# Attention and FFN kernel: w1 moved in two halves, the last batch's rows turned on VectorE, Wq loaded between rows B and C

## The chip, the cores and the metric

The kernel runs on one core of a Trainium2 chip. Its time is that of one launch on the device, in microseconds (us). Five engines work side by side, each through its own list of instructions in order: TensorE (PE; PEld is its loading of weights), VectorE (DVE), ScalarE (ACT), GpSimd (POOL) and SyncE (SP). They wait for one another by semaphores. Transfers are issued by an engine's queue (here SP's and, a few, ACT's) and carried out by 16 DMA engines.

## What is computed

```python
xn = layernorm(x)                                  # x: (8, 1024, 128)
Q = einsum('bnd,hdk->bhnk', xn, proj_q)            # 8 heads
K = einsum('bmd,dk->bmk', xn, proj_k)              # one K and one V for all heads
V = einsum('bmd,dv->bmv', xn, proj_v)
O = softmax(Q @ K.T) @ V
attn = einsum('bhnv,hdv->bnd', O, proj_o)
mid = einsum('amh,ehn->aemn', xn, w1)              # 8 experts, w1: (8, 128, 512)
ffn = einsum('aemn,enh->amh', mid, w2)             # w2: (8, 512, 128)
out = x + attn + ffn
```

All of it is in 32-bit floats. Nothing stands between the two FFN products, so the kernel multiplies w1 and w2 together once, into a 128x128 matrix `wf`. It likewise folds the key projection into the query weights (`wqk`) and the output projection into the values (`wvo`).

## The kernel before, in words

**The unit of work.** The main loop has 512 turns (`for i in range(NS)`): 8 batches of 8 heads of 8 blocks of 128 queries. In turn i, `logits(i)` multiplies the block of queries with all 1024 rows: eight matmuls into a PSUM tile `pl`, of which two exist (tag `sc`, shared with the tiles for queries and values). `exponents(i)` takes the row maximum on VectorE (`nmax`, L359) and the exponents and their sums on ScalarE (`e`, L362). `weights_t(i - 1)` turns the weights of the turn before on VectorE (L394), in 32x32 blocks, into a tile `turned`; `divide(i)` takes the reciprocal of the sums (VectorE, L371) and multiplies (ScalarE, L372).

**From weights to products.** VectorE's transposition works inside 32x32 blocks. Once four turns have filled a `turned` tile (half of a head, 2 MB), `move_blocks` puts the blocks in their places by 16 moves of 32 partitions x 4 KB, issued by SP (L410): the first tile of a head into `g0`, the second into `g1`. There are two buffers of `turned`, two of `g0` and one of `g1`. Twelve turns after a head's first turn (`LAG`), `pair` and `product` multiply `g0`, `g1` and sums of them that GpSimd makes (`f1`, `f4`, L425 to L433) with the values `vf`, into four PSUM banks `acc0` to `acc3` (L455). In the last turns of the kernel TensorE turns the weights instead (`weights_t_pe`).

**Order.** It is written out by hand: every engine gets its instructions in the order in which the program text issues them, and SP's DMAs too stand in one queue in that order.

**The head** (L159 to L173 and the calls before the loop). ACT's queue loads wk, the first head of wq, and the other seven heads (L164). SP's queue loads x_0 in four pieces of two chunks (rows A to D, L163), then wv, wo, w1 (2 MB, into `w1s`, which has the buffer of `g0`) and w2 in two parts. The rows are normalized and turned on TensorE pair by pair (`xn_t_pair`, `pxn`). TensorE turns wq in two groups (`wq_part(1, 4)`, `wq_part(4, 8)`, tile `pwq`) that are copied by ScalarE, multiplies it with wk (`wqk_product`), and does a few products of zeros (`keep_clock`, tile `pidle`). Four PSUM banks are handed out in rotation (`bank`). The rest of the preparation is spread over the first turns by the table `early`.

**w1.** In turns 0 to 3 `turn_w1(k)` turns a quarter of `w1s` on VectorE (L225) into `w1_turned`, part of the buffer of the first values. After the fourth, `load_rows(1)` loads the rows of batch 1 and `move_w1` issues 16 moves of 32 partitions x 4 KB back into `w1s` (L234). In turns 8 to 11 `ffn_weights(k)` multiplies eight of 32 chunks each into `pwf` (bank `acc3`), ScalarE copies the sum (L244), and turn 12 turns it on TensorE (`pwf_t`) and copies it into `wf`.

**Rows of the later batches.** `load_rows(b)` loads them, VectorE takes the moments, GpSimd normalizes. For batches 1 to 6 VectorE turns them (`turn_rows`, L273, one transposition of 1024 columns) and SP moves the blocks in four groups of four moves, four turns apart (`move_rows`, L282). The columns of `xnT` then stand in an order of their own. For the last batch TensorE turns the eight chunks in one go (`xn_t`, L296) and ScalarE copies them (L297), in the natural order.

Of the kernel before, what the change touches and what calls it, by code (L numbers as in the profile page):

```python
# [9 lines left out]
F32 = mybir.dt.float32  # L10
# [7 lines left out]
def kernel(  # L18
# [42 lines left out]
    nc = tc.nc  # L61
    ctx.enter_context(tc.manual_schedule())
    P = 128
# [4 lines left out]
    B, S, D = x.shape  # L68
    H = proj_q.shape[0]
    NE, _, NF = w1.shape  # L70
    NB = S // P
    GN = 4
    GS = GN * P
    NFC = NF // P
    Q = 32
    NQ = P // Q
# [7 lines left out]
    batch = ctx.enter_context(tc.tile_pool(name="batch", bufs=2))  # L84
# [7 lines left out]
    def blocks(t):  # L92
        return t.rearrange("p (c d) -> p c d", d=P)

    def slot(name):
        return ps_sc.tile([P, S], F32, tag="sc", name=name)

    banks, pwf = [0], []

    def both_halves(dst, lhsT, rhs, start=True, stop=True):  # L100
        for half in range(2):
            r = ts(half, HP)
            nc.tensor.matmul(dst[r], lhsT=lhsT[:, r], rhs=rhs, start=start, stop=stop)  # L103

    def bank(name):

        banks[0] = (banks[0] + 1) % (3 if pwf else 4)
        return ps_acc.tile([P, GS], F32, tag=f"acc{banks[0]}", name=name)
# [52 lines left out]
    x_0 = late.tile([P, NB, D], F32, tag="x", name="x_0")  # L161
    for i in range(GN):
        nc.sync.dma_start(x_0[:, ts(i, 2)], chunked(x[0])[:, ts(i, 2)])  # L163
    nc.scalar.dma_start(wq[:, 1:], proj_q[1:].rearrange("h d k -> d h k"))  # L164
    nc.sync.dma_start(wv, proj_v)
    nc.sync.dma_start(wo, proj_o.rearrange("h d v -> d h v"))
    nc.sync.dma_start(w1s.rearrange("p (e n) -> p e n", e=NE), w1.rearrange("e h n -> h e n"))
# [30 lines left out]
    def transposed(dst, srcs, name, copy):  # L198

        pt = blocks(bank(name))  # L200
        for c, src in enumerate(srcs):
            nc.tensor.transpose(pt[:, c, :], src, ident)
        copy(dst, pt[:, : len(srcs), :])

    def wqk_product(first, n):
        pt = blocks(bank(f"pwqk_{first}"))
        if first == 0:
            nc.tensor.matmul(pt[:, 0, :], lhsT=wqT[:, 0, :], rhs=wkT, start=True, stop=True)
        else:
            for c in range(n):  # L210
                both_halves(pt[:, c, :], wqT[:, first + c, :], wkT)
        nc.scalar.copy(wqk[:, first : first + n, :], pt[:, :n, :])
# [4 lines left out]
        nc.scalar.copy(wvo[:, ts(g, GN), :], blocks(pt))  # L217

    wfT = s_v[:, :P]
    w1T = w1s.rearrange("p (r i a) -> p r i a", r=NQ, a=Q)  # L220

    def turn_w1(k):

        i = ts(k, NB)
        nc.vector.transpose(  # L225
            w1_turned.rearrange("p (k i a) -> p i k a", k=NQ, a=Q)[:, i],
            w1s.rearrange("p (i k q) -> p i k q", k=NQ, q=Q)[:, i],
        )

    def move_w1():  # L230
        n = NE * NFC * Q
        for r in range(NQ):
            for k in range(NQ):
                nc.sync.dma_start(w1s[ts(k, Q), ts(r, n)], w1_turned[ts(r, Q), ts(k, n)])  # L234

    def ffn_weights(k):
        if k == 0:
            pwf.append(ps_acc.tile([P, GS], F32, tag="acc3", name="pwf"))
        n = NE * NFC
        for i in range(8 * k, 8 * k + 8):  # L240
            w2_i = w2s[2 * i // n][:, i % (n // 2)]
            both_halves(pwf[0][:, :P], w2_i, w1T[:, :, i, :], i == 0, i == n - 1)
        if k == 3:
            nc.scalar.copy(wfT, pwf.pop()[:, :P])  # L244

# [29 lines left out]
            xns.pop(b).rearrange("p c (k q) -> p c k q", q=Q),  # L275
        )

    def move_quarters(dst, src, r):

        n = S // NQ  # L280
        for k in range(NQ):
            nc.sync.dma_start(dst[ts(k, Q), ts(r, n)], src[ts(r, Q), ts(k, n)])  # L282

    def move_rows(b, r):

        if r == 0:
            xnTs[b] = batch.tile([P, S], F32, tag="xnT", name=f"xnT_{b}")
        move_quarters(xnTs[b], turned_rows[b], r)
        if r == NQ - 1:
            del turned_rows[b]  # L290

    def xn_t(b):
        xnTs[b] = batch.tile([P, S], F32, tag="xnT", name=f"xnT_{b}")
        pt = slot(f"pxn_{b}")
        for c in range(NB):
            nc.tensor.transpose(pt[:, ts(c, P)], xns[b][:, c, :], ident)  # L296
        nc.scalar.copy(xnTs[b], pt)  # L297

    def xn_t_pair(k, copy):

        if k == 0:
            xnTs[0] = batch.tile([P, S], F32, tag="xnT", name="xnT_0")
        pt = bank(f"pxn_0_{k}")
        for c in range(2):
            nc.tensor.transpose(pt[:, ts(c, P)], xns[0][:, 2 * k + c, :], ident)
        copy(xnTs[0][:, ts(k, 2 * P)], pt[:, : 2 * P])

    def queries(u, first=0, last=S, copy=nc.scalar.copy):
        b, h = divmod(u, H)
        if first == 0:  # L310
            qTs[u] = work.tile([P, S], F32, tag="qT", name=f"qT_{u}")
        n = last - first
        pq = slot(f"pq_{u}") if n == S else bank(f"pq_{u}_{first}")
        for c in range(0, n, GS):
            w = min(GS, n - c)
            both_halves(pq[:, c : c + w], wqk[:, h, :], xnTs[b][:, first + c : first + c + w])
        copy(qTs[u][:, first:last], pq[:, :n])  # L317
# [30 lines left out]
    def logits_half(i, g):  # L348
        u, n = divmod(i, NB)
        if g == 0:  # L350
            pls[i] = slot(f"pl_{i}")
        both_halves(
            pls[i][:, ts(g, GS)], qTs[u][:, ts(n, P)], xnTs[u // H][:, ts(g, GS)]
        )
# [293 lines left out]
    def one(t):  # L648
        return t.rearrange("p (c x) -> p c x", c=1)

    def wq_part(first, last):
        transposed(
            wqT[:, first:last], [wq[:, h] for h in range(first, last)], f"pwq_{first}", nc.scalar.copy
        )

    def wo_part(g):
        heads = range(g * GN, (g + 1) * GN)
# [3 lines left out]
    def keep_clock(*widths):  # L661

        for n in widths:
            nc.tensor.matmul(  # L664
                pidle[:, :n], lhsT=idle[:, :P], rhs=idle[:, :n], start=True, stop=True
            )

    def norm_pair(k):
        normalize(0, x_0, nc.vector, (2 * k, 2 * k + 1))

    def stats_pair(k):
# [15 lines left out]
    xn_t_pair(1, nc.scalar.copy)  # L687
    stats_pair(2)
    queries(0, 0, P)
    keep_clock(P)  # L690
    stats_pair(3)
    logits_half(0, 0)
    norm_pair(2)
    xn_t_pair(2, nc.scalar.copy)
    norm_pair(3)
    wq_part(1, 4)
    xn_t_pair(3, nc.vector.tensor_copy)
    logits_half(0, 1)
    wq_part(4, 8)
    queries(0, P, GS)  # L700
    exponents(0)

    early = {
        0: [lambda: wqk_product(1, 3), lambda: queries(0, GS, S)],
        1: [
            lambda: wqk_product(4, 4),
            lambda: queries(1, 0, GS),
# [10 lines left out]
        9: [lambda: ffn_weights(1)],  # L718
        10: [lambda: ffn_weights(2)],
        11: [lambda: ffn_weights(3)],  # L720
        12: [lambda: transposed(one(wf), [wfT], "pwf_t", nc.scalar.copy)],
    }

    PAIRS = (2, 2, 1, 2)
# [24 lines left out]
    for i in range(NS):  # L749
        m = i % GN  # L750
        if i > 0:
            logits(i)
        for task in early.get(i, ()):
            task()
        if 0 <= i - 1 < NS - GN:
            weights_t(i - 1)
        divide(i)
        if i < 4:
            turn_w1(i)
        if i == 3:  # L760
            load_rows(1)
            move_w1()


        v, n = divmod(i - LAG, NB)
        if n == 6 and v + 1 >= 0:
            sum_early(v + 1)


        if i >= LAG:  # L770
            run(PAIRS[m] + (n == 0 and v % H == H // 2 + 1) * 2)
            if n == 0:
                sums_late(v, nc.gpsimd)
        if NS - GN <= i - 1:
            weights_t_pe(i - 1)

        if i % NB == 0 and i > 0 and i // NB + 1 < B * H:
            queries(i // NB + 1)
        if i % NB == GN and i >= LAG:
            s, r = divmod(i + 20, 32)  # L780
            if s < 2 * B:
                values(s, r // NB)


        if i == 8:
            load_x(0)
        if i == NS // B:
            ones_of_last_rows()
        for b in range(1, B):
            r = i - FIRST_ROWS if b == 1 else i - (b - 2) * H * NB - 44  # L790
            if r in ROWS:
                ROWS[r](b)
            r = i - 20 if b == 1 else i - (b - 1) * H * NB
            if b == B - 1:
                if r == 3:
                    xn_t(b)
            elif r in (0, 4, 8, 12):
                if r == 0:
                    turn_rows(b)
                move_rows(b, r // 4)  # L800
        b, r = divmod(i - 23, H * NB)
        if r == 0 and b < B:
            row_diff(b)


        b, r = divmod(i - 69, H * NB)
        if 0 <= b:
            for n in COLLECT.get(r, ()):
                collect(b, n)
            if r in (15, 19, 23, 27):  # L810
                if r == 15:
                    turn_out(b)
                move_out(b, (r - 15) // 4)
            elif r == 36:
                finish(b)
            elif r == 39:
                store(b)
            elif r == 43:
                load_x(b + 1)
# [44 lines left out]
```

## Time and profile before

| | us |
|---|---|
| median of 3 runs (lowest, highest) | 1925.15 (1924.63, 1925.58) |
| the profiled execution | 1924.67 |
| its span, first to last instruction | 1922.9 |
| TensorE busy | 1913.3 |
| SP's issues of `g <- turned`, count; median of one | 2032; 0.590 |
| landing of such a move after its issue, median | 2.4 |
| landing of w1 (2 MB) after its issue | 11.7 |

The profile shows one execution. Its page gives busy times by engine, the chain of work that ended last, and groups of instructions by source line, with the idle time before them and what ended it. Line numbers (L410) are those of the kernel before. A line such as `pl<-xnT,qT` names the tile written and the tiles read. A matmul of 32-bit floats appears as two or more records, and matmuls are pipelined: one lasts longer than the distance from its start to the next one's. A timeline has the start in us from the first instruction, the length of a merged group, engine, line, operation, shapes and count, and in square brackets the idle time before it and what ended it. `SPq` is the issuing of DMAs by SP's queue, not the transfer.

### The profile page before, as it was taken

The page shows a single profiled execution, that of the slowest core. Times are in us where ns is not written, and L with a number is a line of the kernel's source. Part 1 is how long each engine was busy: PE and PEld are TensorE (multiplying, and loading weights), DVE is VectorE, ACT ScalarE, POOL GpSimd, SP SyncE. Part 2 cuts the span into 40 slices and gives each one's busy share as a digit, 9 for nine tenths or more (in the row PEclk, how much of TensorE's full clock was granted, in tenths as well). Part 3 has the DMA queues.
Part 4 walks back from the last instruction along what each step waited for, and adds up shares of the span by engine and source line. Part 5 has one row for each costly group of instructions (what it writes and reads, how often), then busy time and mean ns, then how long its engine had stood idle before and what let it go on. Part 6 is the DMA issues. An engine that isn't in the chain of part 4 may idle for free.

```text
span 1922.9 us, 26882 instructions
## 1 busy us (share of the span) xinstructions
PE 1913.3 (100%) x9037; PEld 665.6 (35%) x9037; DVE 1397.6 (73%) x1774; ACT 1357.4 (71%) x1829; POOL 1405.8 (73%) x593
## 2 busy tenths in 40 slices
PE   9999999999999999999999999999999999999998
PEld 4444443333333333333333333333333333333333
DVE  7767778767786777777777767876777776777775
ACT  7677777777776777777777777776777776777763
POOL 2787777778676886777967778767787676677764
PEclk9999999999999999999999999999999999999999
DMA  7776676676766766677667676666766667567673
GB/s 207 173 157 147 142 155 155 150 164 151 158 144 153 169 155 142 153 159 166 141 154 158 148 176 142 149 153 150 183 139 137 148 155 169 132 143 158 150 166 87
DMA packets 138074, 295.08 MB, mean 153 GB/s; under 512 B 36816, under 2 KB 70352, under 8 KB 137936
## 3 DMA queue, kind: packets, MB, share of 16 engines
q1 hardware_dynamic: 136192, 292.50, 67.8%
q8 instruction: 73, 1.20, 0.3%
q10 hardware_dynamic: 1744, 0.85, 0.2%
q14 instruction: 65, 0.53, 0.1%
HBM read 13.76 MB, written 4.19 MB: 9 GB/s over the span
## 4 chain that ended last, share of the span: by engine, by line
PE 94%; DVE 2%; SPq 2%; ACT 1%; DMA 1%; issue 0%; ACTq 0%; DVEq 0%
PE pl L103 44%; PE acc L455 39%; PE pq L103 5%; PE pv L103 5%; SPq L410 1%; DVE nmax L359 1%; ACT e L362 1%; PE acc L488 1%; SPq L234 0%; DMA g<-turned 0%; DVE turned L394 0%; ACT e L372 0%; DMA scratch_turned<-in_L_attn_proj_q_dram 0%; PE pidle L664 0%; PE pe L383 0%
## 5 line engine op out<-in xcount | busy, mean ns | idle before, releaser
L103 PE MATMUL pl<-xnT,qT 128*64 128x512 f32 x4096 | 968.8, 593 | 2.7 <-ACT e L362 1.6
L359 DVE TENSOR_REDUCE nmax<-pl 128x1 f32<-128x1024 f32 x512 | 626.5, 1224 | 413.3 <-PE pl L103 412.5
L362 ACT ACTIVATE e<-pl,nmax 128x1024 f32<-128x1024 f32 x512 | 570.2, 1114 | 405.5 <-DVE nmax L359 405.5
L455 PE MATMUL acc<-g,vf 128*64 128x512 f32 x2560 | 852.9, 592 | 0.2 <-DMA g<-turned 0.2
L372 ACT ACTIVATE e<-e,rinv 128x1024 f32<-128x1024 f32 x512 | 588.2, 1149 | 120.1 <-DVE rinv L371 120.0
L394 DVE STREAM_TRANSPOSE turned<-e 128x1024 f32<-128x1024 f32 x508 | 628.8, 1238 | 15.1 <-DMA g<-turned 4.3
L103 PEld LDWEIGHTS pl<-xnT,qT 128*64 128x64 f32 x4096 | 299.5, 137 | 579.1 <-issue 528.5
L455 PE MATMUL acc<-f,vf 128*64 128x512 f32 x1016 | 487.2, 592 | 0.0
L430 POOL TENSOR_TENSOR g<-g,g 128x2048 f32<-128x2048 f32 x63 | 286.9, 4555 | 273.7 <-DMA g<-turned 142.7
L455 PEld LDWEIGHTS acc<-g,vf 128*64 128x64 f32 x2560 | 253.0, 137 | 504.4 <-issue 498.8
L425 POOL TENSOR_TENSOR f<-g 128x2048 f32<-128x2048 f32 x63 | 287.0, 4555 | 172.8 <-DMA g<-turned 93.5
L433 POOL TENSOR_TENSOR f<-g,g 128x2048 f32<-128x2048 f32 x63 | 287.3, 4561 | 4.9
L431 POOL TENSOR_TENSOR g<-f,g 128x2048 f32<-128x2048 f32 x63 | 286.8, 4553 | 0.0
L455 PEld LDWEIGHTS acc<-f,vf 128*64 128x64 f32 x1016 | 139.1, 137 | 0.0
L103 PE MATMUL pq<-xnT,wqk 128*64 128x512 f32 (+1 forms) x516 | 121.6, 589 | 0.0
L103 PE MATMUL pv<-wvo,xnT 128*64 128x512 f32 x512 | 120.9, 592 | 0.0
L371 DVE RECIPROCAL rinv<-sums 128x1 f32<-128x1 f32 x512 | 83.9, 164 | 48.5 <-ACT e L362 5.6
L362 ACT ACTIVATION_READ_ACCUMULATOR e<-pl,nmax 128x1 f32 x512 | 98.3, 192 | 0.0
L337 POOL TENSOR_TENSOR vf<-vf 128x256 f32<-128x256 f32 x64 | 46.8, 731 | 28.0 <-ACT vf L336 27.9
L317 ACT COPY qT<-pq 128x1024 f32<-128x1024 f32 (+2 forms) x67 | 64.0, 955 | 0.2 <-PE pq L103 0.2
L103 PEld LDWEIGHTS pv<-wvo,xnT 128*64 128x64 f32 x512 | 37.7, 137 | 72.2 <-issue 68.5
L103 PEld LDWEIGHTS pq<-xnT,wqk 128*64 128x64 f32 x516 | 37.8, 137 | 70.3 <-issue 69.7
(108 smaller groups left out, 536.0 us busy)
## 6 DMA issues: line engine op xcount, KB each, us to landing
g<-turned SPq DMA_DIRECT2D x2032, 128.0 KB, 2.4
xn<-in_L_attn_x_dram SPq DMA_DIRECT2D x7, 512.0 KB, 4.6
out<-yt SPq DMA_DIRECT2D x112, 32.0 KB, 1.9
xnT<-xnt SPq DMA_DIRECT2D x96, 32.0 KB, 1.9
x<-in_L_attn_x_dram SPq DMA_DIRECT2D x6, 512.0 KB, 4.3
out_dram<-x SPq DMA_DIRECT2D x6, 512.0 KB, 5.3
scratch_g<-in_L_ffn_w_dram SPq DMA_DIRECT2D x1, 2048.0 KB, 11.7
scratch_g<-scratch_vf SPq DMA_DIRECT2D x16, 128.0 KB, 2.4
```

The costliest lines, as they stand in the source:

```text
L103: nc.tensor.matmul(dst[r], lhsT=lhsT[:, r], rhs=rhs, start=start, stop=stop)
L317: copy(qTs[u][:, first:last], pq[:, :n])
L359: nc.vector.reduce_max(nmax, pl, AX.X, negate=True)
L362: nc.scalar.activation(es[i], pl, AF.Exp, bias=nmax, accum_out=sums[i])
L371: nc.vector.reciprocal(rinv, sums.pop(i))
L372: nc.scalar.mul(es[i], es[i], rinv)
L394: nc.vector.transpose(turned[k].rearrange("p k c t q -> p c k t q")[:, :, :, j, :], es.pop(i).rearrange("p (c k q) -> p c k q", k=NQ, q=Q),)
L425: nc.gpsimd.tensor_add(f1s[u], key_half(g0s[u], 0), key_half(g0s[u], 1))
L430: engine.tensor_sub(x1, y1, x1)
L431: engine.tensor_sub(x2, f1s[u], y1)
L433: engine.tensor_sub(f4s[u], y2, x2)
L455: nc.tensor.matmul(accs[b, acc][ts(half, HP)], lhsT=vfs[u // GN][:, u % GN, f, c, :], rhs=w[:, :, c, :], start=(h == 0 and c == first), st ...
```

## The change

- The load of the seven heads of wq leaves ACT's queue and stands in SP's, after the second of the four pieces of x_0.
- w1's turned quarters are laid out in two halves. `move_w1(j)` moves one half, 16 moves of 32 partitions x 2 KB: the first in turn 1, after two quarters have been turned, the second in turn 3, after the load of batch 1's rows. The products read w1 by halves.
- `xn_t` goes. The last batch's rows are turned by VectorE and moved by SP at the same turns of the batch as the others', but each piece of 32 columns is put in its natural place, so a move has 256 pieces of 128 B.
- In the head, the first group of wq turns takes the place of one `keep_clock` product, the second stands after the last rows instead of after the second half of the first logits; their copies and the first `wqk_product` are placed accordingly. `pwf_t` moves from turn 12 to turn 13 and takes bank `acc2` by name.

```diff
     for i in range(GN):
         nc.sync.dma_start(x_0[:, ts(i, 2)], chunked(x[0])[:, ts(i, 2)])
-    nc.scalar.dma_start(wq[:, 1:], proj_q[1:].rearrange("h d k -> d h k"))
+        if i == 1:
+            nc.sync.dma_start(wq[:, 1:], proj_q[1:].rearrange("h d k -> d h k"))
...
     def turn_w1(k):
-        i = ts(k, NB)
-        nc.vector.transpose(
-            w1_turned.rearrange("p (k i a) -> p i k a", k=NQ, a=Q)[:, i],
-            w1s.rearrange("p (i k q) -> p i k q", k=NQ, q=Q)[:, i],
-        )
+        j, first = k // 2, k % 2 * NB
+        src = w1s.rearrange("p (i k q) -> p i k q", k=NQ, q=Q)[:, ts(k, NB)]
+        dst = w1_turned.rearrange("p (j k i a) -> p j i k a", j=2, k=NQ, a=Q)
+        nc.vector.transpose(dst[:, j, first : first + NB], src)
 
-    def move_w1():
-        n = NE * NFC * Q
+    def move_w1(j):
+        n = NE * NFC * Q // 2
         for r in range(NQ):
             for k in range(NQ):
-                nc.sync.dma_start(w1s[ts(k, Q), ts(r, n)], w1_turned[ts(r, Q), ts(k, n)])
+                nc.sync.dma_start(
+                    w1s[ts(k, Q), ts(j * NQ + r, n)], w1_turned[ts(r, Q), ts(j * NQ + k, n)]
+                )
...
         for k in range(NQ):
-            nc.sync.dma_start(dst[ts(k, Q), ts(r, n)], src[ts(r, Q), ts(k, n)])
+            dst, src = xnTs[b][ts(k, Q)], turned_rows[b][ts(r, Q), ts(k, n)]
+            if b < B - 1:
+                nc.sync.dma_start(dst[:, ts(r, n)], src)
+            else:
+                dst = dst.rearrange("p (c r q) -> p r c q", r=NQ, q=Q)[:, r]
+                nc.sync.dma_start(dst, src.rearrange("p (c q) -> p c q", q=Q))
...
     queries(0, 0, P)
-    keep_clock(P)
+    turn_wq(1, 4)
     stats_pair(3)
     logits_half(0, 0)
+    copy_wq(1, 4)
     norm_pair(2)
     xn_t_pair(2, nc.scalar.copy)
     norm_pair(3)
-    wq_part(1, 4)
     xn_t_pair(3, nc.vector.tensor_copy)
+    turn_wq(4, 8)
     logits_half(0, 1)
-    wq_part(4, 8)
+    copy_wq(4, 8)
+    wqk_product(1, 3)
     queries(0, P, GS)
     exponents(0)
 
+    def turn_wf():
+        pt = ps_acc.tile([P, P], F32, tag="acc2", name="pwf_t")
+        nc.tensor.transpose(pt, wfT, ident)
+        nc.scalar.copy(wf, pt)
...
-        0: [lambda: wqk_product(1, 3), lambda: queries(0, GS, S)],
+        0: [lambda: queries(0, GS, S)],
...
-        12: [lambda: transposed(one(wf), [wfT], "pwf_t", nc.scalar.copy)],
+        13: [turn_wf],
...
         if i < 4:
             turn_w1(i)
+        if i == 1:
+            move_w1(0)
         if i == 3:
             load_rows(1)
-            move_w1()
+            move_w1(1)
...
-            if b == B - 1:
-                if r == 3:
-                    xn_t(b)
-            elif r in (0, 4, 8, 12):
+            if r in (0, 4, 8, 12):
                 if r == 0:
                     turn_rows(b)
                 move_rows(b, r // 4)
```

More of the change, by code (lines that the diff above doesn't have):

```diff
@@ L219 @@
     wfT = s_v[:, :P]
-    w1T = w1s.rearrange("p (r i a) -> p r i a", r=NQ, a=Q)
+    w1T = w1s.rearrange("p (j r i a) -> p j r i a", j=2, r=NQ, a=Q)
     def turn_w1(k):
-        i = ts(k, NB)
-        nc.vector.transpose(
-            w1_turned.rearrange("p (k i a) -> p i k a", k=NQ, a=Q)[:, i],
-            w1s.rearrange("p (i k q) -> p i k q", k=NQ, q=Q)[:, i],
-        )
-    def move_w1():
-        n = NE * NFC * Q
+        j, first = k // 2, k % 2 * NB
[4 more added lines that the diff above has]
+        n = NE * NFC * Q // 2
         for r in range(NQ):
             for k in range(NQ):
-                nc.sync.dma_start(w1s[ts(k, Q), ts(r, n)], w1_turned[ts(r, Q), ts(k, n)])
+                nc.sync.dma_start(
+                    w1s[ts(k, Q), ts(j * NQ + r, n)], w1_turned[ts(r, Q), ts(j * NQ + k, n)]
+                )
     def ffn_weights(k):
@@ L241, in ffn_weights @@
             w2_i = w2s[2 * i // n][:, i % (n // 2)]
-            both_halves(pwf[0][:, :P], w2_i, w1T[:, :, i, :], i == 0, i == n - 1)
+            both_halves(pwf[0][:, :P], w2_i, w1T[:, 2 * i // n, :, i % (n // 2), :], i == 0, i == n - 1)
         if k == 3:
@@ L276, in turn_rows @@
         )
-    def move_quarters(dst, src, r):
-        n = S // NQ
-        for k in range(NQ):
-            nc.sync.dma_start(dst[ts(k, Q), ts(r, n)], src[ts(r, Q), ts(k, n)])
     def move_rows(b, r):
@@ L287, in move_rows @@
             xnTs[b] = batch.tile([P, S], F32, tag="xnT", name=f"xnT_{b}")
-        move_quarters(xnTs[b], turned_rows[b], r)
+        n = S // NQ
+        for k in range(NQ):
+            dst, src = xnTs[b][ts(k, Q)], turned_rows[b][ts(r, Q), ts(k, n)]
[4 more added lines that the diff above has]
+                nc.sync.dma_start(dst, src.rearrange("p (c q) -> p c q", q=Q))
         if r == NQ - 1:
             del turned_rows[b]
[L292 to L297, printed above, removed]
     def xn_t_pair(k, copy):
@@ L649, in one, with turn_wq, copy_wq @@
         return t.rearrange("p (c x) -> p c x", c=1)
[L651 to L654, printed above, removed]
+    pwqs = {}
+    def turn_wq(first, last):
+        pwqs[first] = blocks(bank(f"pwq_{first}"))
+        for h in range(first, last):
+            nc.tensor.transpose(pwqs[first][:, h - first, :], wq[:, h], ident)
+    def copy_wq(first, last):
+        nc.scalar.copy(wqT[:, first:last], pwqs.pop(first)[:, : last - first])
     def wo_part(g):
```

## The prediction

> **What bounds the kernel now.** I read part 1 of the page, then what TensorE waited for, then the stretch from 15 to 66 us engine by engine. Part 1:
>
> ```profile
> PE 1913.3 (100%) x9037; PEld 665.6 (35%) x9037; DVE 1397.6 (73%) x1774; ACT 1357.4 (71%) x1829; POOL 1405.8 (73%) x593
> ```
>
> TensorE is busy for all but some 10 us of 1922.9. So a matmul that goes is worth its own length, and any other edit only matters where TensorE stands still. The view of waits on TensorE names those places (us in total, times, longest):
>
> ```profile
> PE pl L103 <- ACT e L362: 1.6, 2, 1.0
> PE pwf_t L202 <- ACT scratch_vf L244: 0.8, 1, 0.8
> PE pl L103 <- DVE xnT L306: 0.6, 1, 0.6
> ```
>
> One `pl` wait of 1.0 lies at 1891, at the end. The other, and `pwf_t`'s, lie in turns 12 and 13 of the main loop. The timeline of TensorE there (start, length, what, idle before):
>
> ```profile
> 53.80 1.95 PE L103 MATMUL pwf<-scratch_g,scratch_f 128*64 128x128 f32 x32
> 56.32 1.94 PE L103 MATMUL pl<-xnT,qT 128*64 128x512 f32 x8 [0.57 <-ACT e L362]
> 59.03 0.33 PE L202 MATMUL pwf_t<-ident,scratch_vf 128*128 128x128 f32 x1 [0.78 <-ACT scratch_vf L244]
> 59.56 1.94 PE L455 MATMUL acc<-g,vf 128*64 128x512 f32 x8 [0.20 <-DMA g<-turned]
> ```
>
> A `pl` or a `pwf` group normally takes 1.72 us from its start to the next one's, so `pl` at 56.32 is 0.80 late (53.80 + 1.72 = 55.52) and `pwf_t` 1.0 late (56.32 + 1.72 = 58.04). Both wait for ScalarE, and ScalarE waits for VectorE, whose timeline shows the cause:
>
> ```profile
> 47.11 1.23 DVE L359 TENSOR_REDUCE nmax<-pl 128x1 f32<-128x1024 f32 x1 [1.43 <-PE pl L103]
> 52.61 1.25 DVE L394 STREAM_TRANSPOSE turned<-e 128x1024 f32<-128x1024 f32 x1 [4.28 <-DMA g<-turned]
> ```
>
> The transpose at 52.61 is that of turn 8 (I call it T8). It writes `turned_2`, the third of four-turn tiles in a pool of two buffers, so it needs the buffer of `turned_0`, and that is free when the 16 moves `g0 <- turned_0` have landed. The last of them landed at 52.20. They stand in SP's queue, in order:
>
> ```profile
> 15.34 5.27 SPq L124 DMA_DIRECT2D xn<-in_L_attn_x_dram  x1
> 29.27 10.11 SPq L234 DMA_DIRECT2D scratch_g<-scratch_vf  x16
> 39.48 22.29 SPq L410 DMA_DIRECT2D g<-turned  x32
> ```
>
> SP idles from 20.6 to 29.27 (it waits for the fourth turn of w1), then issues 16 moves of w1 and 32 of `g` without a gap, 0.635 us each. **That queue sets the one stall of the main loop**, and the change rewrites it.
>
> **w1 in two halves.** 16 moves of 128 KB become 32 of 64 KB. The price of one is that of its issue: moves of 128 KB have a median of 0.590 us, those of 32 KB (`xnT <- xnt`, also 32 rows) 0.589, so I take 0.635 with the gap for 64 KB too. The sum for SP's queue:
> - Start: after turn 2 of w1, which ended at 20.78. The load of w1 landed at 15.59 and the transpose started at 15.61, so w1's landing leads here, not TensorE; I take 20.7.
> - First half, 16 moves: 10.16 (29.27 to 39.43 in this trace), to 30.86.
> - The load of xn_1 now comes here: 0.63 (the six later ones issue in 0.58 to 0.59), to 31.49. It lands by about 36 (4.6 to landing) and is read at 44.4, so the move itself is free.
> - Second half: 10.16, to 41.65. SP's moves to `g0`: 0.05, then as now 10.93 with one slow issue of 1.40, to 52.63. The last is issued at 51.98, against 49.76 now: 2.2 later.
>
> The halves are needed by `pwf` at turns 8 and 10 (41.67 and 50.34) and land by 33.3 and 44.1: no stall there, and none was there before. So the split removes no wait of TensorE and puts 17 more issues (10.8 us) before `g0` into a hole of 8.6.
>
> Then comes a second delay. At 43.3 and 53.0 the instruction queue of part 3 fetches 16 KB, every 250 or so TensorE instructions; both times the SP issue at that moment took 1.40 and 1.83 us instead of 0.59, and the moves issued up to 1.3 us before it landed late (issued 51.67 and 52.31: 4.07 and 3.75 us to landing, not 2.4). Now the second fetch hits `g1`, which has time. After the change TensorE reaches that instruction at about 53.0 - 0.92 (its lead, below) + 0.4 (four instructions fewer before it, at 0.107) = 52.5, half a us after the last `g0` move is issued. That move then lands like the one at 52.31, 3.06 after the fetch: 55.56. T8 starts 0.41 after the landing, as now (52.20 to 52.61): 55.97. **T8 is 3.36 late**; without the hit it is 51.98 + 2.85 = 54.83, 2.2 late.
>
> What follows T8 (reciprocals, exponents, the copy of `pwf`) moves with it. TensorE's `pl` goes from 56.32 to 59.68. `pwf_t` leaves turn 12, but the `acc` product in its place takes `acc3`, the bank of `pwf`, so it still waits for the copy at L244 and starts at 59.03 + 3.36 instead of 59.56 + 3.36: 0.53 gained. `pwf_t` comes back in turn 13 for about 0.2 (eight transposes took 1.12, plus an edge). Sum of turns 8 to 13: 3.36 - 0.53 + 0.20 = **+3.03**. The products with `g1` then start at 67.8; its last move lands by 66, and `f1` and `x1` on GpSimd have over 2 us left, so nothing else becomes late.
>
> **Head of the kernel.** wq's load leaves ACT's queue (0.46, ahead of a table load that ends at 3.45, while ScalarE's first work starts at 4.35 behind VectorE: nothing) and enters SP's between rows B and C (0.52). Rows C and D, wv, wo, w1 and w2 are issued 0.5 later. Rows C and D landed at 6.52 and 7.40, sharing the engines with wq, which landed at 8.13. Behind wq the same bytes are 448 + 128 + 128 KB from about 3.8 on; at 250 to 310 KB a us they end at 6.1 to 6.7: not later than now, so no cost; if they came 0.5 later, the lead below shrinks by that. TensorE: the spare matmul at 7.98 becomes three turns of wq in the same wait for ScalarE; `pxn_3` comes forward over `pwq` (-0.33: 9.92 instead of 10.25), and four turns of wq move from after `pl` into the wait before it (-0.59: 12.24 to 12.83). TensorE leads by 0.92 from turn 1. That lead is worth nothing: it ends in the wait for T8, which TensorE does not set. The price of the cover is in the third rival.
>
> **Last batch.** Eight transposes on TensorE go:
>
> ```profile
> 1440.90 0.59 PE L455 MATMUL acc<-f,vf 128*64 128x512 f32 x1
> 1441.43 1.09 PE L296 MATMUL pxn<-ident,xn 128*128 128x128 f32 x8
> 1442.45 1.94 PE L103 MATMUL pl<-xnT,qT 128*64 128x512 f32 x8
> ```
>
> Without them `pl` starts at 1440.90 + 0.43 = 1441.33: **-1.12**, all of it TensorE's own time. A copy of 0.99 on ScalarE goes with them. One transpose of 1.25 on VectorE and 16 moves on SP come; the batch before has just these at 1200 to 1254, and TensorE is busy 15.00 of 15.00 us there. The last batch writes its rows in pieces of 128 B, 256 to a move; no data piece in this trace is so small. Nearest row: the 256 pieces of 512 B of `x` (L139) issue in 0.45 to 0.58, no dearer. Upper end: 1.86, the slowest `xnT` move, for all 16; SP's stretches there are almost full (0.3 to 2.9 us free of 15), and a group's moves have some 3.6 us to spare before the transpose two groups on, so this end costs up to 2 us. I take 0, by the nearest row; first reader is turn 428, 120 us after the last move. [...]
>
> **Sum.** +3.03 - 1.12 = +1.91. Against the profiled execution (1924.67, span 1922.9) 1926.6; the median of the runs is 0.48 above it, so 1925.15 + 1.9 = **1927.1**. That is 0.1%; a measurement of this kernel tells apart about 0.2%, 3.85 us.
>
> **Rivals.**
> 1. *The fetch misses the last `g0` moves.* T8 2.2 late: 2.2 - 0.33 - 1.12 = +0.75, 1925.9. The hit rests on an estimate good to half a us. If the slow issue of 1.40 also falls elsewhere, -0.1: 1925.0. Chance 0.33.
> 2. *The clock falls* (slower). TensorE would stand from 54.83 (55.75 now, less 0.92) to 59.68, 4.85 us. This trace shows what a pause does (window, length, PE, PEld, DVE, ACT, POOL, granted clock, DMA, GB/s):
>
> ```profile
> 1918.40:1921.70 3.30, 0.00 (x0) 0.00 (x0) 0.42 (x2) 0.00 (x0) 0.00 (x0) 1.00 0.58 161
> 1921.80:1922.80 1.00, 0.00 (x0) 0.00 (x0) 0.00 (x0) 0.00 (x0) 0.00 (x0) 0.50 0.00 0
> ```
>
>    The last matmul ends at 1918.34 and 3.43 later the clock is at half. At half clock `pl` takes 1.72 more, of which 1.0 lies in the wait for `pwf`'s copy: 0.7. At the start full clock came at 6.9, 5.6 us after the first matmul (1.31); so until 65.3 or, one such wait longer, 69, half of what follows 63.1 is lost: 1.1 to 2.9. In all +3.7 to +5.5: 1928.9 to 1930.7, say 1929.5. It decides from a pause of 3.43 on. For it: 4.85 is longer. Against it: one row, at the end, and with the fetch missed the pause is 3.7. [...] Chance 0.24.
> 3. *An issue costs by its bytes* (faster). The halves then take 0.34 each: 20.7 + 5.4 + 0.63 + 5.4 + 11 = 43.1, T8 is on time, the stalls of 0.80, 1.0 and 0.44 (59.12 to 59.56) go and the lead of 0.92 stays: -3.16 + 0.2 - 1.12 = -4.1, 1921.1. Against it: 0.590 for 128 KB, 0.589 for 32 KB. Chance 0.03.
> 4. *The small pieces of the last batch hold up SP*: +1.9 to +3.9, 1928. Chance 0.05.
>
> **Numbers.** Forecast 0.35; rivals 0.33, 0.24, 0.03, 0.05. Faster by over 0.2% only in rival 3: 0.03. Slower by over 0.2% in somewhat over half of rival 2: 0.13. Same 0.84. Range 1924.6 (rival 1 at its low end, less the spread of the runs) to 1929.6 (middle of rival 2).
>
> **What would show it.** SP's L234 row in two blocks of some 10 us from 20.7 and 31.5; `g <- turned` from 41.7; T8 at 56 (54.8 in rival 1, 48 in rival 3) after a wait of about 9 on `g<-turned`; TensorE's wait before turn 12's `pl` near 4.8; the granted clock under 1 near 59 in rival 2; no `pxn` at 1441. I am wrong if SP's pitch for 64 KB isn't 0.63 or T8 starts by 53.

## The result, and the profile after

The changed kernel takes **1927.74 us** (median of 22 runs, 1926.76 to 1929.21) against 1925.12 before (22 runs beside them, 1924.23 to 1926.59): a ratio of 1.0014, 95% interval 1.0008 to 1.002. That is 2.6 us slower, below the 0.2% that the prediction set as its bound, and inside its range. The profiled execution took 1927.64, its span 1925.7.

Part 1 of the page of the changed kernel, and then what TensorE waited for (us in total, times, longest):

```profile
PE 1912.1 (99%) x9027; PEld 648.8 (34%) x9027; DVE 1397.8 (73%) x1775; ACT 1357.0 (70%) x1828; POOL 1407.0 (73%) x593
```

```profile
PE pl L103 <- ACT e L359: 6.6, 2, 5.6
PE pidle L666 <- POOL idle L176: 1.3, 1, 1.3
PE pl L103 <- ACT qT L314: 0.9, 1, 0.9
```

TensorE has 1.2 us less to do than before, and yet the kernel is slower: one wait for `e` has grown from 0.6 to 5.6, and `pwf_t`'s wait is gone from the list. The timeline of TensorE shows the place:

```profile
52.75 1.92 PE L103 MATMUL pwf<-scratch_g,scratch_f 128*64 128x128 f32 x32
60.23 3.48 PE L103 MATMUL pl<-xnT,qT 128*64 128x512 f32 x8 [5.56 <-ACT e L359]
63.54 1.88 PE L452 MATMUL acc<-g,vf 128*64 128x512 f32 x8
...
68.78 0.33 PE L709 MATMUL pwf_t<-ident,scratch_vf 128*128 128x128 f32 x1
69.04 1.94 PE L452 MATMUL acc<-g,vf 128*64 128x512 f32 x8
```

`pl` of turn 12 starts at 60.23 (56.32 before) and takes 3.48 instead of 1.94: the clock is at half. VectorE and SP show why TensorE stood, T8 first, then SP's queue:

```profile
56.53 1.25 DVE L391 STREAM_TRANSPOSE turned<-e 128x1024 f32<-128x1024 f32 x1 [9.26 <-DMA g<-turned]
```

```profile
20.67 10.38 SPq L234 DMA_DIRECT2D scratch_g<-scratch_vf  x16
31.10 0.58 SPq L124 DMA_DIRECT2D xn<-in_L_attn_x_dram  x1
31.78 11.36 SPq L234 DMA_DIRECT2D scratch_g<-scratch_vf  x16
43.24 21.56 SPq L407 DMA_DIRECT2D g<-turned  x32
```

SP starts w1 where the prediction put it (20.67 for 20.7) and needs 22.5 us for the two halves and the load between them, where the prediction had 20.95; `g0` begins at 43.24, 3.8 later than before, and T8 is 3.92 late. From turn 14 on TensorE is 4.36 behind the kernel before.

The last batch, in the same timeline, has no `pxn` left before `pl` of turn 388 (it stood at 1441.43 before, ahead of that `pl` at 1442.45):

```profile
1445.26 0.59 PE L452 MATMUL acc<-f,vf 128*64 128x512 f32 x1
1445.68 1.89 PE L103 MATMUL pl<-xnT,qT 128*64 128x512 f32 x8
```

There 1.13 comes back (4.36 behind up to turn 387, 3.23 at turn 388), 0.05 more at turn 389, and nothing else moves up to the last `pl`.

The clock, by its rows. From the profile of the changed kernel (window, length, PE, PEld, DVE, ACT and POOL busy with counts, granted clock, DMA share, GB/s), in stretches of 3.41:

```profile
53.12:56.53 3.41, 1.55 (x30) 1.31 (x24) 0.00 (x1) 0.00 (x0) 0.00 (x0) 1.00 0.67 148
56.54:59.95 3.41, 0.00 (x0) 0.00 (x0) 3.31 (x4) 2.10 (x2) 3.41 (x1) 1.00 0.95 209
59.96:63.36 3.40, 3.13 (x8) 0.98 (x10) 2.87 (x5) 3.10 (x7) 1.09 (x1) 0.50 0.87 195
63.37:66.78 3.41, 3.41 (x18) 1.12 (x16) 2.87 (x6) 2.28 (x4) 0.00 (x0) 1.00 0.83 194
```

The stretch without matmuls (56.54 to 59.95) is followed by one at half clock (0.50), and that one, with 3.13 of 3.40 us of matmuls, by full clock (1.00). So what the prediction held for its second rival, a fall of the clock, happened here. By the mean granted clock it happened in most or all of the runs: that is 0.998 in 15 of the 22, 0.999 in 7 and 1.0 in none, against 1.0 in 25 of 33 runs of the kernel before and 0.999 in the other 8. The profile above, with one stretch at half clock, has 0.999, and a second profile with two (run 7) has 0.998; the 15 runs at 0.998 have a median of 1927.89, the 7 at 0.999 one of 1927.18.

### The profile page after: what moved, and what is told of

Read it like the earlier page. It is cut to its first block, busy times and chain, and to the rows that moved or that the text cites. A ratio compares the mean times of both kernels' runs of the same rounds, so it can differ in the third digit from the quotient of the medians.

```text
span 1925.7 us, 26898 instructions
## 1 busy us (share of the span) xinstructions
PE 1912.1 (99%) x9027; PEld 648.8 (34%) x9027; DVE 1397.8 (73%) x1775; ACT 1357.0 (70%) x1828; POOL 1407.0 (73%) x593
## 4 chain that ended last, share of the span: by engine, by line
PE 82%; POOL 6%; SPq 4%; DVE 3%; DMA 2%; ACT 2%; issue 1%; POOLq 0%; DVEq 0%
PE pl L103 38%; PE acc L452 33%; PE pv L103 5%; PE pq L103 5%; SPq L407 4%; DVE nmax L356 2%; POOL f L430 2%; POOL g L427 2%; POOL g L428 2%; DMA g<-turned 2%; ACT e L359 1%; DVE turned L391 1%; PE acc L485 1%; ACT e L369 1%; DMA x<-in_L_attn_x_dram 0%
## 5 line engine op out<-in xcount | busy, mean ns | idle before, releaser
L103 PEld LDWEIGHTS pl<-xnT,qT 128*64 128x64 f32 x4096 | 292.6, 137 | 592.8 <-issue 534.8
```

## The experiments

My theory after the result: the two halves hold SP's queue longer, that makes T8 late, and the instruction fetches (at 39.4 and 52.2 in the first profile, where SP's issues took 1.89 and 1.63 us) and the fall of the clock (to 0.50 from 59.95 to 63.36) add to it; the head's lead is worth nothing, and the last batch gives back 1.1. The rivals stand with each run. The kernel before, run beside them, has a median of 1925.13 for 1 to 4 and 1924.95 for 5, 8, 9 and 10; medians of versions are of 9 to 11 runs, 6, 7 and the second of 8 are single runs.

**1. The halves alone**, in the kernel before (with the layouts in `turn_w1`, `move_w1` and `ffn_weights` that they need):

```diff
+        if i == 1:
+            move_w1(0)
         if i == 3:
             load_rows(1)
-            move_w1()
+            move_w1(1)
```

> The kernel before with the two halves of w1 alone. Theory of the queue (SP's queue sets T8, the transpose of turn 8, and T8 sets TensorE): SP starts w1 at 20.8, the last g0 move goes out near 54, T8 starts at 56 to 57 against 52.6, pl of turn 12 at 60 against 56.3. TensorE has no lead here and pwf_t stays in turn 12, so nothing is given back: 3.5 to 4.5 slower than before, 1928.6 to 1929.6. Rival (the loss comes from the small pieces of the last batch or from wq in SP's queue): within 0.5 of before.

Measured: 1929.11, ratio 1.002 (1.0011 to 1.0028), 4.0 slower than before. Its TensorE, in the timeline:

```profile
60.52 3.37 PE L103 MATMUL pl<-xnT,qT 128*64 128x512 f32 x8 [5.05 <-ACT e L363]
63.82 0.47 PE L202 MATMUL pwf_t<-ident,scratch_vf 128*128 128x128 f32 x1
```

`pl` is 4.20 later than before, exactly as much as T8 (56.81 against 52.61), and 0.51 more is lost behind it at half clock. The halves are the whole loss. Of the 11 runs one has a mean clock of 1.0; it took 1927.13, the shortest.

**2. The change with w1 moved whole** behind the fourth turn and in the layouts of before:

```diff
-        if i == 1:
-            move_w1(0)
         if i == 3:
             load_rows(1)
-            move_w1(1)
+            move_w1()
```

> The changed kernel with w1 moved whole after turn 3, as before. Theory of the queue: T8 back at 52.6 within 0.4, the acc product of turn 12 starts 0.3 to 0.5 earlier than before, pwf_t costs 0.2 to 0.3 in turn 13, and the transposes of the last batch are saved: 1.3 to 1.5 faster than before, near 1923.7. No fall of the clock at turn 12, since the pause there is under 3. Rival (small pieces or wq): 1926 or more.

Measured: 1922.65, ratio 0.9987 (0.9978 to 0.9996), 2.5 faster than before and 5.1 faster than the change. From its timeline:

```profile
55.16 1.94 PE L103 MATMUL pl<-xnT,qT 128*64 128x512 f32 x8
57.92 1.94 PE L451 MATMUL acc<-g,vf 128*64 128x512 f32 x8 [0.82 <-issue]
```

The long wait is gone (`pl` is still 0.32 late, `acc` 1.04) and the clock stays at 1.0. I had expected 1.4 and got 2.5. SP starts w1 at 28.54 instead of 29.27, since the fourth turn of w1 follows TensorE's lead, and T8 comes at 51.46 instead of 52.61. With w1 whole, the lead is worth something.

**3. The last batch's rows alone**, in the kernel before: `xn_t` goes, `move_rows` as in the change.

```diff
-            if b == B - 1:
-                if r == 3:
-                    xn_t(b)
-            elif r in (0, 4, 8, 12):
+            if r in (0, 4, 8, 12):
```

> The kernel before with the last batch's rows on VectorE and SP alone. Theory: 1.1 faster than before (the 1.12 of TensorE's transposes), 1924.0; the head and T8 as before. Rival (moves of 256 pieces of 128 B hold up SP and with it the g moves): same as before or slower, with a wait of TensorE or of a turned transpose near turns 385 to 405.

Measured: 1923.55, ratio 0.9993 (0.9984 to 1.0002), 1.6 faster than before; in its profile `pl` of turn 388 gains 1.12 on the turns before it. The interval reaches 1, so the profile carries this, not the time.

**4. The clock held up**: the change, with five products of zeros in TensorE's pause, into a free bank. They compute nothing that is used.

```diff
-        11: [lambda: ffn_weights(3)],
+        11: [lambda: ffn_weights(3), lambda: hold_clock(5)],
```

> The changed kernel with five products of zeros (128x128x512) on TensorE behind the last pwf group of turn 11, into a bank that is free then; their results are not used. They fill some 4.3 of the pause before turn 12's pl, so the clock has no reason to fall. Theory: T8 and pl of turn 12 as in the changed kernel (within 0.3 apart from the fetches), granted clock 1.0 throughout; the profile of the changed kernel gives the fall 0.5 to 0.6, so 0.3 to 0.7 faster than the changed kernel, near 1927.2. Rival (the fall of the clock is the main cost): 1.5 or more faster, 1926.2 or less.

Measured: 1926.42, ratio 1.0009 (1.0 to 1.0017), 1.3 faster than the change: between what I expected and the rival. The mean clock is 1.0 in 10 of the 11 runs. From its timeline:

```profile
54.87 4.56 PE L715 MATMUL phold<-idle 128*128 128x512 f32 x10
59.86 1.94 PE L103 MATMUL pl<-xnT,qT 128*64 128x512 f32 x8 [0.43 <-ACT e L359]
62.62 1.94 PE L452 MATMUL acc<-g,vf 128*64 128x512 f32 x8 [0.82 <-issue]
```

`pl` still starts 3.70 behind T8, as wherever it waits for T8 (59.86 and 56.16), but takes 1.94, and `acc` follows 2.76 after it instead of 3.31. The fall seems to cost more than the 0.5 of the one profile I had; run 7 says why. The 1.3 is not all shown to be the clock's: T8 differs by 0.37 between these two profiles, and the intervals of the two ratios overlap.

**5. Fewer TensorE instructions before turn 12**, for the instruction fetch: in the change, spare matmuls at the start merged, and seven of the `wqk` products as one full matmul instead of two halves.

```diff
-                both_halves(pt[:, c, :], wqT[:, first + c, :], wkT)
+                nc.tensor.matmul(pt[:, c, :], lhsT=wqT[:, first + c, :], rhs=wkT, start=True, stop=True)
...
-    keep_clock(P, P, P)
+    keep_clock(3 * P)
...
-    keep_clock(P, P)
+    keep_clock(2 * P)
```

> The changed kernel with some 40 fewer TensorE instructions before turn 12: the spare matmuls of the start merged into fewer, wider ones, and seven heads' wqk products as one full-width matmul each instead of two half-width ones. The arithmetic that counts is the same. Theory: TensorE's instruction fetch, one per some 250 instructions, slows the issue of SP's DMAs and the landing of those under way; in the changed kernel's trace it comes at 52.2, on the last moves to g0. With 40 instructions fewer it comes after 54.5, when those moves are issued; T8 then starts at 55.2 to 55.6 instead of 56.53, and the kernel is about 1.0 us faster than the changed kernel (1926.5 to 1926.8 where that has 1927.7). Rival: the fetch is a coincidence and the slow issue comes from the queue itself: T8 and the time as in the changed kernel, within 0.3.

Measured: 1926.69, ratio 1.0011 (1.0002 to 1.002), 1.05 below the change's median. But the profiled execution took 1929.72: T8 at 57.85, and half clock for two stretches. So the time came as I expected and the trace did not show the reason. A second profile follows.

**6. The same once more.**

> The version with fewer TensorE instructions, profiled a second time: its first profiled execution took 1929.7 us where the median of its runs was 1926.7, so its trace does not show a usual run. Theory: in a usual run the third fetch comes at 54.5 to 55, after the last g0 move has landed or just on it, T8 starts at 55.2 to 56.2, TensorE's pause is under 5 and the time 1926.2 to 1927. Rival: the fetch still holds up the last g0 move, T8 at 57 or later as in the first profile, and the lower median comes from elsewhere.

Measured: 1927.70. T8 at 55.43 and a pause of 3.74, as expected; the time was not, again with two stretches at half clock. The last move of `g0` and the fetch, in five profiles (us):

| profile | issued | next fetch | landed | issue to landing |
|---|---|---|---|---|
| before | 49.76 | 53.0 | 52.20 | 2.4 |
| changed kernel, again (run 7) | 50.83 | 51.5 | 54.26 | 3.43 |
| fewer instructions | 53.52 | 54.9 | 57.44 | 3.91 |
| fewer instructions, again | 52.59 | 55.3 | 55.01 | 2.43 |
| changed kernel | 53.74, after an issue of 1.63 at 52.07 | 52.2, before it | 56.11 | 2.38 |

The two moves that landed before the fetch took 2.4 and 2.43; the two that were on their way when it came took 3.43 and 3.91; in the first profile of the change the fetch came earlier, at 52.2, and there SP's issue took 1.63 instead of 0.59. That the fetch came some 3 us later is seen; that it is the cause of the lower median is not shown, because in the two profiles T8 is not earlier than in the two of the change. Part of the lower median goes with the clock: 7 of the 11 runs have a mean clock of 0.999 (median 1926.63), 3 have 0.998 and one 0.997, where the change has 0.999 in 7 of 22. Among the runs at 0.999 this version is still 0.55 below the change (1927.18), for which no run shows a cause.

**7. The changed kernel once more.**

> The changed kernel once more, for how much T8, the fetches and the clock's fall differ between two executions of one program: T8 56.0 to 57.0, third fetch at 52 to 53, half clock for one window of 3.4 us, time 1927 to 1928.5. If T8 or the length of the half clock differ by more than that, the differences of under 1 us between the profiles of versions say nothing.

Measured: 1927.84, as expected. T8 came at 54.68, 1.85 before the first profile, the third fetch at 51.5, and two stretches were at half clock: all three outside what I expected. The first fetch came at 17.3, before SP's moves, w1 began at 19.77, and the second half took 10.67 instead of 11.36. The span, 1924.9, is shorter by only 0.8 and not by 1.85, for the clock (the time of the launch is no shorter at all: 2.9 lie around the span here, 1.9 in the first profile):

```profile
53.33:56.73 3.40, 0.96 (x18) 0.72 (x14) 2.05 (x3) 0.73 (x1) 2.04 (x1) 1.00 0.85 188
56.74:60.14 3.40, 1.76 (x4) 0.53 (x6) 3.21 (x5) 3.17 (x5) 2.47 (x1) 0.50 0.90 200
60.15:63.55 3.40, 3.40 (x10) 0.92 (x8) 2.37 (x4) 2.22 (x5) 0.00 (x0) 0.50 0.86 192
63.57:66.97 3.40, 3.40 (x18) 1.12 (x16) 2.18 (x8) 2.16 (x3) 1.74 (x1) 1.00 0.91 229
```

Two stretches at half clock instead of one: the pause of 4.09 ends in the middle of the second stretch, which holds 1.76 us of matmuls, and the third is still at 0.50. From `pl` of turn 12 to that of turn 13 it takes 7.76, against 6.74 in the first profile and 6.21 at full clock (runs 2 and 8). So the fall cost 0.53 with one stretch and 1.55 with two in these profiles, and the 1.3 of run 4 lies between. The other profiles agree: 0.51 with one stretch in run 1, 1.48 and 1.88 with two in runs 5 and 6. My warning on record holds too: single profiles of this kernel differ by more than 1 us in T8, so versions are compared by medians, and profiles term by term.

**8. The head's changes alone**, in the kernel before: wq's load in SP's queue, its turns moved, `pwf_t` in turn 13.

```diff
-    nc.scalar.dma_start(wq[:, 1:], proj_q[1:].rearrange("h d k -> d h k"))
+        if i == 1:
+            nc.sync.dma_start(wq[:, 1:], proj_q[1:].rearrange("h d k -> d h k"))
...
-        12: [lambda: transposed(one(wf), [wfT], "pwf_t", nc.scalar.copy)],
+        13: [turn_wf],
```

> The kernel before with only the head's changes: wq's load in SP's queue between rows B and C, the turns of wq moved into TensorE's waits, pwf_t in turn 13. w1 is moved whole behind its fourth turn and the last batch's rows are turned on TensorE, as before. Theory: TensorE's lead of 0.8 to 0.9 brings w1's fourth turn, SP's start and so T8 forward with it: T8 at some 51.5 instead of 52.6, turns 13 and 14 about 1.2 earlier, the time about 1.2 below before: 1923.9. Rival (the step on record, that the lead is worth nothing): T8 as before, the time within 0.3 of before, 1924.8 to 1925.4.

Measured: 1924.29, ratio 0.9997 (0.9988 to 1.0006): 0.66 below before, half of what I expected and more than the rival; by the interval it is no difference. In the profiled execution the full clock came late, at 10.13, and the first `pl` 1.3 late. Once more:

> The version with the head's changes alone, profiled a second time: in its first profile the full clock came at 10.1 us instead of 5 to 7 and the first logits were 1.3 late, and its time was 1.3 over the median of its runs. Theory: with the clock up by 7.7, TensorE leads by 0.8 to 0.9 from turn 1, SP starts w1's moves at 28.5, T8 comes at 51.5 to 52.2, and the time is 1924.0 to 1924.4. Rival: SP starts no earlier than before (29.2) and T8 is as before (52.6).

Measured: 1924.20. SP and VectorE in that second profile:

```profile
28.61 10.13 SPq L235 DMA_DIRECT2D scratch_g<-scratch_vf  x16
```

```profile
52.15 1.25 DVE L395 STREAM_TRANSPOSE turned<-e 128x1024 f32<-128x1024 f32 x1 [4.46 <-DMA g<-turned]
```

The time, SP's start and T8 are as expected, the lead is a little smaller. SP starts 0.66 earlier than before with TensorE's lead of 0.69, T8 is 0.46 earlier, and the turns from 14 on are 0.51 earlier. The lead reaches T8, less some tenths on the way.

**9 and 10. w1 whole, but earlier.** If SP's start sets T8, an earlier start should take the stall away. The version of run 2, with the four turns of w1 in three turns of the loop, once as 1, 1, 2 and once as 1, 2, 1:

```diff
-        if i < 4:
-            turn_w1(i)
-        if i == 3:
+        for k in ((0,), (1,), (2, 3))[i] if i < 3 else ():
+            turn_w1(k)
+        if i == 2:
             load_rows(1)
             move_w1()
```

> As the version before, with the quarters of w1 turned one in turn 0, one in turn 1 and two in turn 2 and the moves behind these. Theory: SP starts w1 at some 25.6, T8 at 48.4 to 49.7; VectorE's second quarter now delays the row maximum of turn 3, by when TensorE has a turn more in hand: the same time or slightly better than one-two-one, 1921.2 to 1922.0. Rival: VectorE's crowding costs TensorE directly, 1922.6 to 1923.7.

> The version with w1 moved whole (changed head and last batch) with the quarters of w1 turned one in turn 0, two in turn 1, one in turn 2, and the load of xn_1 and the 16 moves behind turn 2 instead of turn 3. Theory: SP's start of w1's moves sets T8 and so turns 8 to 13. SP starts at some 25.7 instead of 28.5, T8 comes at 48.4 to 49.7 instead of 51.5, and TensorE no longer waits in turn 12 (pl at some 54.8). Against it, VectorE's second quarter in turn 1 delays the row maximum of turn 2 by about 1.1 and may take up to 0.5 of TensorE's lead. Time 0.5 to 1.4 us below the version with w1 moved whole: 1921.3 to 1922.2. Rival: what is left in turns 12 and 13 there is not SP's doing, and VectorE's crowding in turns 1 and 2 costs TensorE directly: same as that version or up to 1 slower (1922.6 to 1923.7).

Measured: 1, 1, 2 takes **1920.28**, ratio 0.9977 (0.9967 to 0.9987), the fastest of all, faster than I expected; 1, 2, 1 takes 1921.25, ratio 0.9981 (0.9972 to 0.999), as expected. The timeline of TensorE for 1, 1, 2:

```profile
52.66 1.92 PE L103 MATMUL pwf<-scratch_g,scratch_f 128*64 128x128 f32 x32
54.41 1.89 PE L103 MATMUL pl<-xnT,qT 128*64 128x512 f32 x8
56.12 1.93 PE L451 MATMUL acc<-g,vf 128*64 128x512 f32 x8
57.86 1.92 PE L103 MATMUL pv<-wvo,xnT 128*64 128x512 f32 x8
```

No wait is left there: each group starts 1.71 to 1.75 after the one before. SP starts w1 at 25.24, T8 comes at 49.66, and TensorE keeps its lead (1.14 at turn 9). With 1, 2, 1 it is 0.45 behind there, and its timeline shows two waits that 1, 1, 2 does not have:

```profile
20.49 1.08 PE L103 MATMUL pq<-xnT,wqk 128*64 128x512 f32 x4 [0.30 <-ACT wqk L213]
...
25.79 1.94 PE L103 MATMUL pv<-wvo,xnT 128*64 128x512 f32 x8 [0.63 <-ACT wvo L218]
```

VectorE's second quarter comes a turn earlier there (2.35 us for two, from 20.08), and the row maximum behind it at 22.35; that ScalarE's copies are late through this I read from the order of the engines and did not try.

## Why the prediction was right or wrong

Forecast 1927.1, measured 1927.74. The parts of its sum, beside the two profiles of the changed kernel (us against the profile of before; the first is that of the result, the second that of run 7):

| term | predicted | first | second |
|---|---|---|---|
| T8 | +3.36 | +3.92 | +2.07 |
| `pwf_t` out of turn 12 | -0.53 | -0.49 | -0.49 |
| fall of the clock | 0 (rival 2) | +0.53 | +1.55 |
| `pwf_t` in turn 13 | +0.20 | +0.41 | +0.41 |
| turns 8 to 13 | +3.03 | +4.36 | +3.54 |
| last batch | -1.12 | -1.13 | -1.12 |
| last `pl` (turn 511) | +1.91 | +3.18 | +2.37 |

- **SP's queue sets the stall: right.** A move of 64 KB had a pitch of 0.633 and an issue of 0.589 (median of 32), as taken from the rows of 128 and 32 KB; it landed in about 2.0 instead of 2.4, which helped no one. Rival 3 falls. Undoing the halves takes the long wait away (run 2), and an earlier start of the same queue takes away what was left of the stall (run 9).
- **T8: right in kind, 0.56 too small in the first profile and 1.29 too large in the second.** I counted one slow issue of 1.40 in SP's `g0` and one hit of the fetch at 52.5 on the landing of the last move. The fetch I had at 43.3 came at 39.4 and 39.2, in the second half of w1: an issue of 1.89 in the first profile, 1.20 in the second. In the first profile an issue of 0.86 followed the fetch at 20.6, and the one at 52.2 hit SP's issue (1.63) instead of the last landing; so the last `g0` move went out at 53.74 instead of 51.98 and landed 2.38 later instead of 3.58. In the second SP began 0.93 earlier than I took (w1 landed at 14.73 instead of 15.59), the last move went out at 50.83, and the fetch at 51.5 hit its landing (3.43). Rival 1 (the fetch misses) did not occur in these two profiles.
- **The fall of the clock is the step that failed.** The prediction gave it a chance of 0.24, an estimate, "from a pause of 3.43 on", at 1.8 to 3.6 on top of the forecast. It happened in both profiles (0.50 from 59.95 to 63.36 in the first, from 56.74 to 63.55 in the second), by the mean clock in most or all runs, and at 0.53 to 1.55. The 3.43 was one reading, from the end of the kernel before, and these runs did not repeat it: from the end of the last matmul to the fall it took 5.28 us in the first profile, 2.44 in run 7, 2.76 in run 6 and 5.4 in run 1, with pauses of 5.56, 4.09, 3.74 and 5.05. In the rows by stretches of 3.41, the one just before the half clock held 0.00 us of matmuls (the first profile), 0.96 (run 7), 0.66 (run 6) and 0.34 (run 1); after 1.55 (the first profile) and 1.41 (run 1), one stretch earlier, the clock was still at 1.00. The pause of the forecast, 4.85, lies among those after which it fell. The price was too high: I let full clock come back only 5.6 us after `pl` began, as at the start, or 9.3; it came 3.13 after it in the first profile and 5.17 in the second.
- **`pwf_t`: right in turn 12** (0.49 for 0.53), too cheap in turn 13: 0.41, since `pl` of turn 14 starts 3.84 after that of turn 13 instead of 3.43; run 2 and run 8, at full clock, show 3.87.
- **The lead of the head: 0.92 predicted, 1.02 and 1.29 measured at turn 1; worth nothing, right with the halves.** Halves (+3.98) and rows (-1.58) alone add to +2.40, and all three together are +2.62, so the head gives nothing there that these medians show, and SP starts w1 at 20.67 with the lead and at 20.71 without it (run 1). It is not so with w1 whole (-0.66 alone, runs 2 and 8): there the fourth turn of w1 and with it SP's start follow the lead. The prediction did not say this, as it priced only the kernel with the halves.
- **wq in SP's queue: right in its worth, not in its times.** wq landed at 6.59 instead of 8.13, rows C and D at 7.01 and 7.46, not at the forecast 6.1 to 6.7 but 0.49 and 0.06 later than before. The lead did not shrink by it.
- **Last batch: right to a hundredth.** Rival 4 falls: four moves in pieces of 128 B issue in 2.60 to 2.66 instead of the 2.44 to 2.50 of the batch before it in the old kernel, and each lands in 1.92 to 2.5 instead of 1.82 to 2.02. So the smaller pieces cost here some 0.04 us a move in issue and 0.1 to 0.5 to landing, and no one waits.

The loss of the halves and the gain of the last batch were right in kind and about in size. That the sum came within 0.6 is in part luck: a term left at nothing (the clock, +0.5 to +1.5) meets, in the second profile, one that is too large (T8, 3.36 for 2.07). How much each makes of the median of 1927.74 stays open, since two profiles are not 22 runs, and so does a part of what made the version with fewer instructions 1 us faster.

## What to carry to other kernels

Here, where an issuing queue was the limit, splitting a transfer to start it sooner cost one issue for each piece (0.589 us for 64 KB, 0.590 for 128 KB), and everything behind it in the queue paid (`g0` began 3.8 later); leaving it whole and starting it a turn sooner (1, 1, 2) was 4.7 us faster than the kernel before, leaving it whole alone 2.5 (1920.28 against 1924.95, 1922.65 against 1925.13). Count what an earlier step brings forward, not only what it saves on its own path. Pauses of TensorE of 3.74 to 6.33 us cost this kernel 0.5 to 1.9 us more by the clock (0.50 for one or two stretches of 3.41), and a forecast has to price it.

## What the runs showed of the hardware

- In the profiles of before and of the change, the instruction queue (q8 in part 3 of the page) fetched 16 KB 73 and 72 times, for 9037 and 9027 matmul records and as many weight loads of TensorE: one for some 250 of them. The 54 and 55 issues of SP during which such a fetch began (after 19 us) had a median of 1.45 and 1.52 us, the others one of 0.589. Of SP's 60 and 61 issues above 0.8 us, 57 and 59 held the start of a fetch or began within 0.9 us of one. The moves of `g` in whose first 2.0 us a fetch began landed after 3.63 and 3.65 us (median of 185 and of 187), the others after 2.38. These are coincidences in time; no run shows a cause behind them.
- At half clock, stretches of 3.40 with 1.76 (run 7) and 2.42 us of matmuls (run 6) were followed by another at 0.50, and those with 3.13 (the first profile), 3.39 (run 1) and 3.40 (runs 6 and 7) by one at 1.00.
- One program lost one stretch in one execution (59.95 to 63.36, first profile of the change) and two in another (56.74 to 63.55, run 7). Full clock began nearly alike in the two (5.34 and 5.54), and it was the end of the pause that moved (60.23 and 58.38). In the first profile the changes at 59.95, 63.36 and 1923.63 come 16, 17 and 562 times 3.4133 us after 5.34; in the profile of before the one at 1921.77 comes 561 times 3.4133 after 6.90. No run shows what sets the number of stretches.
